# Layer 3's last mixture of experts: order of the last batch's routing and dense units, and bf16 products for its gate and up

## The chip, the core and the metric

The kernel runs on one core of a Trainium2 chip. The core has TensorE (PE, with its weight loads shown apart as PEld), VectorE (DVE), ScalarE (ACT), GpSimd (POOL) and SyncE (SP), each with an instruction queue of its own that runs in order. DMAs are issued by SP and by GpSimd. The metric is the device time of one execution in microseconds; lower is better.

## The reference

Four batches of 512 tokens, 128 wide, go through four layers of self-attention, cross-attention and a feed-forward part, each with a residual. The change concerns the last feed-forward part, a mixture of 32 experts of inner width 64, four per token, with a capacity of 256 rows per expert counted over all four batches in order, and one shared expert. Its weights are drawn as bf16 numbers.

```python
logits = (X @ gate_w.T).astype(jnp.float32)
scores = jax.nn.sigmoid(logits)
_, idx = jax.lax.top_k(scores + bias[None, :], K)
w = jnp.take_along_axis(scores, idx, axis=-1)
w = w / jnp.clip(jnp.sum(w, axis=-1, keepdims=True), 1e-12, None)
...
pos = jnp.take_along_axis(jnp.cumsum(onehot, axis=0) - 1, eid[:, None], axis=1)[:, 0]
valid = pos < C
...
h = jax.nn.silu(jnp.einsum('ecd,edi->eci', xe, W1)) * jnp.einsum('ecd,edi->eci', xe, W3)
ye = jnp.einsum('eci,eid->ecd', h, W2)
gflat = jnp.where(valid, w.reshape(-1), jnp.zeros((), x.dtype))
yrows = ye[eid, posc] * gflat[:, None]
out = yrows.reshape(-1, K, D).sum(axis=1)
out = out + jax.nn.silu(X @ sw1.T) * (X @ sw3.T) @ sw2.T
```

## The kernel before

Tokens are kept as rows (`x`, 128 partitions) and, after a layer norm, transposed in `xT` (128 x 512 per batch, `tokens(b)`). All products of this part are f32.

Batches 0, 1 and 2 go through **slots**. `route_slots` (L737) computes the routing on VectorE (`capped`, L686, with `router` and `topk`), and GpSimd scatters each token's row to its four experts' slots in DRAM, 16 indirect DMAs per batch (L776). This happens while the cross-attention before it still runs. `slot_experts` (L813) then fetches the slots of four half-experts at a time into SBUF: eight DMAs on SP (L825), which wait for all scatters. Eight rounds follow, each of four phases that lag behind each other: `turn` (four transposes, L830, and a ScalarE copy, L832), `inner` (four gate-and-up products at L425, SiLU on ScalarE at L846, a product on VectorE), `inner_turn` (two transposes, L854, a copy on VectorE, L856) and `down` (four products at L425, scaled by the token's weight on ScalarE, L870, and VectorE, L871). Each round ends in four indirect DMAs of GpSimd that scatter the rows back to a buffer `back` in DRAM (L873), 32 in all. `returned` (L912) fetches that buffer with three DMAs on SP (L919), adds the rows to `x` in 12 VectorE additions and stores each batch (L930). The shared expert of batches 0 to 2 is `shared_rows` (L895).

Batch 3 is **dense**: `ffn` (L951) runs every token through all experts, in 17 units of two experts each (the first unit is the shared expert). A unit is a gate and an up product (L425, to two PSUM banks `f`), SiLU on ScalarE (L1005), two VectorE products at L436 (by up, then by the routing weights spread over partitions), and, two units later, a down product (L1013) into the bank `acc`. The spread is a bf16 product of a pick matrix and the weights in three bf16 parts (`spread3`, L886); they come from `route_dense` (L717). PSUM has four banks `f`, one `acc`, three `s`.

The program is written as generators. `weave` (L390) steps one chain and takes a step of a second one every so many steps. Within what the program's order and dependencies leave open, a scheduler sets the order of each engine; inside `manual_schedule` the order of VectorE is the written one. In the last part the order is: shared rows of batches 0 and 1, then the rounds taking turns with the shared rows of batch 2, with batch 3's norm and routing woven in at one step per 2.2; then all 17 dense units, with the returned rows' additions woven in; then the last sums and batch 3's store (`out`, L2173).

Six weight packs hold gate, up and down of the 17 units as f32 in SBUF. Since the source in DRAM is bf16, `load` (L370) has GpSimd issue those DMAs, which convert; three of the six are in GpSimd's queue behind the scatters of batch 2. Loads without a conversion go to SP's queue. The room of the attention's tiles is given to this part once the attention is through.

Of the kernel before, what the change touches and what calls it, by code (L numbers as in the profile page):

```python
# [13 lines left out]
F32 = mybir.dt.float32  # L14
BF16 = mybir.dt.bfloat16
# [3 lines left out]
ALU = mybir.AluOpType  # L19
# [3 lines left out]
P = 128  # L23
B, S, D = 4, 512, 128
# [267 lines left out]
class Net:  # L292
# [74 lines left out]
    def acc(self, shape=(P, 512)):  # L367
        return self.bank("acc", shape)

    def load(self, name, pool, tag, cols=None):  # L370
        at, n = self.packs[name]
        src = self.dram[name]
        t = pool.tile([P, cols or n], F32, tag=tag, name="w_" + name.replace(".", "_"))
        cast = src.dtype != F32
        (self.nc.gpsimd if cast else self.nc.sync).dma_start(t[:, :n], src)
        return Weights(t, at)

# [275 lines left out]
    def spread(self, w, group, away, pool):  # L653

        nc = self.nc
        T, E = w.shape[1], w.shape[2]
        wp = pool.tile([P, T, E], F32, name="w_halves", tag="w_halves", bufs=1)
        nc.gpsimd.tensor_copy(
            wp.rearrange("p t (h u) -> p t h u", h=2), w.rearrange("p t (u h) -> p t h u", h=2)
        )  # L660
        yield
        for i, b in enumerate(group):
            t = self.sm((E, S))
            for j in range(TB):
                nc.tensor.transpose(t[:, j * P : j * P + P], wp[:, TB * i + j, :], self.ident)
            wT = pool.tile([E, S], F32, tag="w_turned", name="w_turned", bufs=2)
            self.move(wT, t)
            nc.sync.dma_start(away[b], wT)
            yield
# [16 lines left out]
    def capped(self, b, W, pool, m):  # L686
# [27 lines left out]
        nc.vector.scalar_tensor_tensor(fits, pp, float(CAP), hit, ALU.is_lt, ALU.mult)  # L714
        self.tt(w, w, fits, ALU.mult)

    def route_dense(self, b, W, pool):  # L717

        nc = self.nc
        E = 32  # L720
        m = {}
        yield from self.capped(b, W, pool, m)
        yield
        w3, rest = pool.tile([P, TB, 3, E], BF16, name="w3", bufs=1), pool.tile([P, TB, E], F32, name="w_rest", bufs=1)
        nc.vector.tensor_copy(w3[:, :, 0], m["w"])
        self.tt(rest, m["w"], w3[:, :, 0], ALU.subtract)
        nc.vector.tensor_copy(w3[:, :, 1], rest)
        self.tt(w3[:, :, 2], rest, w3[:, :, 1], ALU.subtract)
        yield
        t = self.bank("s", [3 * E, S], BF16)  # L730
        for j in range(TB):
            nc.tensor.transpose(t[:, j * P : j * P + P], w3[:, j].rearrange("p k e -> p (k e)"), self.identb)
        self.w3T = pool.tile([3 * E, S], BF16, name="w3T", bufs=1)
        nc.scalar.copy(self.w3T, t)
        yield
# [215 lines left out]
    def ffn(self, stage, group, E, base, pool, spread=None):  # L951

        nc = self.nc
        packs = self.units_of(stage, group)
        blocks = [packs[i : i + 2] for i in range(0, len(packs), 2)]
        away = self.chunks[stage] if not spread else None
        rest = [(b, [int(u) for u in routed]) for blk in blocks for b in group for _, _, routed in blk if routed]
        coming = []  # L960

        def chunk():

            if not rest or spread:
                return
            b, units = rest.pop(0)
            c = pool.tile([P, UNITS, S], F32, tag="c", name="c", bufs=3)
            for h in range(2):
                first = h * E // 2 + units[0]
                src = away[b, first : first + len(units)].rearrange("e s -> (e s)")  # L970
                nc.sync.dma_start(
                    c[64 * h : 64 * h + 64, : len(units)].rearrange("p e s -> p (e s)"), src.partition_broadcast(64)
                )
            coming.append(c)

        y = {b: pool.tile([P, S], F32, tag="y", name="y", bufs=4) for b in group}
        self.sums.update({(stage, b): y[b] for b in group})
        chunk()
        chunk()
        at = base  # L980
        for k, blk in enumerate(blocks):
            Ws = [self.pack(at + i, n) for i, (n, _, _) in enumerate(blk)]
            at += len(blk)
            ahead = at + len(blocks[k + 1]) - 1 if k + 1 < len(blocks) else at + 1
            for b in group:
                units = [(W, u, None) for W, (_, sh, _) in zip(Ws, blk) for u in sh]
                plan = []
                for W, (_, sh, routed) in zip(Ws, blk):
                    plan += [(W, u, None) for u in sh] + [(W, u, i) for i, u in enumerate(routed)]
                acc, cs = {}, {}  # L990
                for i, (W, u, in_c) in enumerate(plan):
                    if in_c is not None and spread:
                        if u not in cs:
                            cs.update(spread([v for _, v, in_c in plan[i : i + 2] if in_c is not None]))
                        cu = cs.pop(u)
                    elif in_c is not None:
                        if in_c == 0:
                            chunk()
                            c = coming.pop(0)
                        cu = c[:, in_c, :]  # L1000
                    pg, up = self.bank("f", (P, S)), self.bank("f", (P, S))
                    self.dot(pg, (W["g" + u], self.tokens(b)))
                    self.dot(up, (W["u" + u], self.tokens(b)))
                    h = pool.tile([P, S], F32, tag="h", name="h", bufs=5)
                    nc.scalar.activation(h, pg, AF.Silu)  # L1005
                    self.tt(h, h, up, ALU.mult)
                    if in_c is not None:
                        self.tt(h, h, cu, ALU.mult)

                    def down(W=W, u=u, h=h, i=i, b=b, acc=acc, n=len(plan), k=k):  # L1010
                        if i == 0:
                            acc["t"] = self.acc()
                        nc.tensor.matmul(acc["t"], lhsT=W["d" + u], rhs=h, start=i == 0, stop=i == n - 1)  # L1013
                        if i == n - 1 and k == 0:
                            nc.scalar.copy(y[b], acc["t"])
                        elif i == n - 1:
                            self.tt(y[b], y[b], acc["t"], ALU.add)

                    self.last.append(down)
                    if len(self.last) > 2:  # L1020
                        self.last.pop(0)()
                    if b == group[0] and i == 2:
                        self.want(ahead)
                    yield
# [13 lines left out]
    def l0_attn(self, pool, W, Wo):  # L1038
# [199 lines left out]
        def rounds(first, last):  # L1238
            n = len(items)
            item = lambda i: items[i] if 0 <= i < n else None  # L1240
            if first == 0:
                yield from project(0)
                load(0, 0)
                biases()
                load(0, 1)
                yield
# [932 lines left out]
def chained(*chains):  # L2179
    for c in chains:  # L2180
        yield from c


def some(steps, n):

    for _ in range(n):
        if next(steps, steps) is steps:
            return
        yield


def build(nc, packs, dram):
    first, second = GROUPS
    of = lambda stage: [n for n in packs if n.startswith(stage + ".") and n[-1].isdigit()]
    f2 = [f"l2_ffn.{kind}{hp}" for hp in range(8) for kind in ("qkv", "o")]
    feed = ["l0_attn.qk", "l0_attn.vo"]
    at = {}
# [6 lines left out]
    with tile.TileContext(nc) as tc, ExitStack() as ctx:  # L2204
        net = Net(ctx, tc, packs, dram, feed)
# [3 lines left out]
        def open_pool(name, right=False):  # L2209
            pools[name] = ExitStack()  # L2210
            return pools[name].enter_context(net.pool(name, right=right))
# [29 lines left out]
        ff = open_pool("ff")  # L2241
# [20 lines left out]
        y = {b: gates.tile([P, S], F32, name=f"y{b}") for b in range(B)}  # L2262
# [38 lines left out]
        dense = lambda b, fast=False: net.l2_dense(b, y[b], w4, s4, fast)  # L2301
# [17 lines left out]
        s5 = open_pool("s5", right=True)  # L2319
        x3 = open_pool("x3")  # L2320
# [15 lines left out]
        W5 = Both()  # L2336
# [11 lines left out]
        ff = open_pool("ff3")  # L2348
        banks(f=4, acc=1, s=3)
        net.want(at["l3"] + 2)  # L2350
        for i, n in enumerate(of("l3_ffn")):
            net.stay[n] = net.loaded[at["l3"] + i] if i < 3 else net.load(n, ff, f"w{i}")
        chain = chained(net.norm(3), net.route_dense(3, W5, s5))
        shared = [net.shared_rows(b, net.stay[of("l3_ffn")[0]], ff) for b in range(3)]
        net.weave(chained(shared[0], shared[1], net.turns(net.slot_experts(at["l3"], ff), shared[2])), chain, 2.2)
        with tc.manual_schedule(engines={mybir.EngineType.DVE}):
            back = net.returned(range(3), ff)
            next(back)
            net.weave(net.ffn("l3_ffn", (3,), 32, at["l3"], ff, net.spread3), back, 1.5, 6)
        net.flush()  # L2360
        for _ in net.out(3):
            pass
# [22 lines left out]
```

## Time and profile before

| What | us |
|---|---|
| median of three runs (2251.18 to 2261.61) | 2256.95 |
| the profiled execution, its own time | 2272.79 |
| its span, first to last instruction | 2271.0 |
| last scatter of batch 2 to the slots starts (L776) | at 2152.29 |
| first slot transposes on PE (L830) | at 2161.03 |
| first and last scatter back (L873) | at 2174.34 and 2224.72 |
| fetch of the returned rows (L919) | at 2226.86 |
| first store of the output (L930) | at 2243.07 |

Times of events are counted from the start of the span. A line number is that of the kernel before; L425 is `dot` and L436 `tt`, the helpers that record most products and most VectorE operations, so the tiles tell what such a row is: `f<-xT,w_l_ffn` is a gate or up product, `s<-w3T,pick` the spread, `acc<-h,w_l_ffn` the down product, `made` the scaled rows of a round. An f32 product of 512 columns appears as two MATMUL records, each with a weight load; a bf16 one as one. The ends of matmuls are modelled, so their starts are the safer measure. "Idle before" is the time in which an engine stood still ahead of an instruction, with what ended it; "remote" is a release whose source the profile doesn't know.

### The profile page before, as it was taken

What the parts mean: (1) busy time and instruction counts of PE and PEld (TensorE: products, weight loads), DVE (VectorE), ACT (ScalarE), POOL (GpSimd) and SP (SyncE); (2) the same over time, 40 slices, a digit from 0 to 9 for tenths busy, and PEclk for the clock granted to TensorE, in tenths of its full rate; (3) what the DMA queues carried; (4) which work ended last, traced back from release to release, by engine and by line L of the source; (5) the groups of instructions that cost most, each with busy time, mean ns of one, the idle gap of its engine ahead of it and who ended that gap; (6) DMA issues with size and microseconds to landing.
All of it is one profiled execution on the core that took longest, in us unless ns stands there. A gap on an engine that the chain in (4) does not pass through costs nothing.

```text
span 2271.0 us, 28138 instructions
## 1 busy us (share of the span) xinstructions
PE 2109.5 (93%) x8946; PEld 1121.5 (49%) x8946; DVE 1608.1 (71%) x4059; ACT 995.4 (44%) x2042; POOL 554.8 (24%) x695
## 2 busy tenths in 40 slices
PE   6999899999999998999999999999999996697778
PEld 3566556544545553444444544444444443564463
DVE  6667576666675769787977797867777765886525
ACT  4556446444325452444434543443343434364421
POOL 1000001000000001433323343333333322336541
PEclk7989999999999999999999999999999998898869
DMA  6321134254453344334334444444443442200022
GB/s 167 99 65 44 45 111 123 62 137 112 112 143 84 105 101 107 75 100 110 110 83 105 114 120 114 124 111 107 114 114 101 111 129 46 94 1 6 20 54 76
DMA packets 88947, 213.26 MB, mean 94 GB/s; under 512 B 21874, under 2 KB 40626, under 8 KB 88542
## 3 DMA queue, kind: packets, MB, share of 16 engines
q1 hardware_dynamic: 85230, 207.52, 34.9%
q0 software_dynamic: 3568, 3.93, 0.6%
q8 instruction: 71, 1.16, 0.2%
q14 instruction: 78, 0.64, 0.1%
HBM read 182.33 MB, written 23.53 MB: 91 GB/s over the span
## 4 chain that ended last, share of the span: by engine, by line
PE 72%; DVE 15%; issue 5%; ACT 3%; POOL 2%; DMA 2%; SPq 1%; another core or an unknown queue 0%; POOLq 0%; DVEq 0%; ACTq 0%
PE mm L425 19%; PE f L425 13%; PE mm L1854 8%; PE s L425 8%; PE acc L1013 6%; PE mm L1826 4%; PE mm L1801 4%; DVE h L436 2%; PE mm L1136 1%; PE mm L1203 1%; PE mm L1181 1%; DVE at_m L1883 1%; DVE m L1143 1%; DVE gvx L436 1%; PE s L515 1%
## 5 line engine op out<-in xcount | busy, mean ns | idle before, releaser
L1762 POOL TENSOR_TENSOR gvx<-gvx 128x512 f32<-128x512 f32 (+1 forms) x256 | 260.3, 1017 | 549.3 <-DVE gvx L436 488.3
L425 PE MATMUL f<-xT,w_l_ffn 128*128 128x512 f32 (+1 forms) x768 | 369.3, 603 | 1.2 <-ACT h L1005 0.7
L1885 ACT ACTIVATE at_e<-mm,at_m 128x512 f32<-128x512 f32 x256 | 173.0, 685 | 293.1 <-DVE at_m L1883 274.3
L425 PE MATMUL mm<-w_l_ffn_qkv,xT 128*128 128x512 f32 x512 | 266.3, 604 | 4.2 <-ACT at_e L1885 1.7
L1854 PE MATMUL mm<-og,w_l_ffn_o 128*128 128x512 f32 x512 | 265.8, 603 | 3.2 <-DVE og L436 3.2
L436 DVE TENSOR_TENSOR h<-h,f 128x512 f32<-128x512 f32 (+1 forms) x192 | 131.1, 684 | 139.9 <-PE f L425 105.3
L1005 ACT ACTIVATE h<-f 128x512 f32<-128x512 f32 x189 | 112.3, 596 | 251.0 <-PE f L425 214.2
L425 PEld LDWEIGHTS f<-xT,w_l_ffn 128*128 128x128 f32 (+1 forms) x768 | 140.2, 192 | 151.0 <-issue 123.6
L1013 PE MATMUL acc<-h,w_l_ffn 128*128 128x512 f32 x378 | 194.8, 600 | 3.5 <-DVE h L436 2.9
L436 DVE TENSOR_TENSOR gvx<-mm,gv 128x512 f32<-128x512 f32 x256 | 174.5, 683 | 20.8 <-PE mm L425 17.1
L436 DVE TENSOR_TENSOR og<-mm,c 128x512 f32<-128x512 f32 x256 | 176.2, 690 | 18.3 <-PE mm L1854 16.0
L1802 ACT COPY eT<-mm 128x512 f32<-128x512 f32 x256 | 137.6, 596 | 83.4 <-PE mm L1801 83.2
L1883 DVE TENSOR_REDUCE at_m<-mm 128x1 f32<-128x512 f32 x256 | 161.1, 681 | 11.7 <-PE mm L425 10.3
L1801 PEld LDWEIGHTS mm<-ident,at_e 128*128 128x128 f32 x1024 | 120.2, 142 | 68.4 <-issue 47.7
L1854 PEld LDWEIGHTS mm<-og,w_l_ffn_o 128*128 128x128 f32 x512 | 91.7, 191 | 114.4 <-issue 90.3
L1801 PE MATMUL mm<-ident,at_e 128*128 128x128 f32 x1024 | 135.1, 274 | 5.3 <-ACT at_e L1885 5.3
L425 PEld LDWEIGHTS mm<-w_l_ffn_qkv,xT 128*128 128x128 f32 x512 | 87.3, 190 | 95.2 <-issue 59.0
L425 PE MATMUL mm<-roped 64*128 64x512 f32 x512 | 131.3, 622 | 1.7 <-DVE roped L436 1.0
L1143 DVE TENSOR_REDUCE m<-mm 128x1 f32<-128x512 f32 (+3 forms) x176 | 104.8, 635 | 32.6 <-PE mm L1139 31.7
L1826 PE MATMUL mm<-eT,v 128*64 128x512 f32 x512 | 118.7, 599 | 0.0
L1013 PEld LDWEIGHTS acc<-h,w_l_ffn 128*128 128x128 f32 x378 | 71.2, 192 | 93.1 <-issue 67.3
L436 DVE TENSOR_TENSOR h<-h,c 128x512 f32<-128x512 f32 x160 | 111.5, 703 | 4.1 <-DMA c<-l_ffn_w 1.3
(453 smaller groups left out, 3529.4 us busy)
## 6 DMA issues: line engine op xcount, KB each, us to landing
c<-gates SPq DMA_DIRECT2D x256, 256.0 KB
c<-l_ffn_w SPq DMA_DIRECT2D x96, 384.0 KB
w_l_ffn<-in_l_ffn SPq DMA_DIRECT2D x26, 576.0 KB
w_l_ffn_qkv<-in_l_ffn_qkv SPq DMA_DIRECT2D x16, 640.0 KB
w_l_ffn_o<-in_l_ffn_o SPq DMA_DIRECT2D x16, 512.0 KB
rot<-qk SPq DMA_DIRECT2D x128, 64.0 KB
d<-inverted SPq DMA_DIRECT2D x64, 128.0 KB
k_parts<-k SPq DMA_DIRECT2D x12, 384.0 KB
```

The costliest lines, as they stand in the source:

```text
L425: self.nc.tensor.matmul(out, lhsT=lhsT, rhs=rhs, start=i == 0, stop=i == len(pairs) - 1)
L436: self.nc.vector.tensor_tensor(out, a, b, op)
L1005: nc.scalar.activation(h, pg, AF.Silu)
L1013: nc.tensor.matmul(acc["t"], lhsT=W["d" + u], rhs=h, start=i == 0, stop=i == n - 1)
L1143: nc.vector.tensor_reduce(m[:, i, h0 : h0 + per], ps, AX.X, ALU.max, negate=True)
L1762: nc.gpsimd.tensor_tensor(x[:, :, :m], x[:, :, :m], x[:, :, m : 2 * m], ALU.add)
L1801: nc.tensor.transpose(p[:, j, :], es[i][hl][:, j * P : j * P + P], self.ident)
L1802: nc.scalar.copy(eT[hl][:, :, i * P : i * P + P], p)
L1826: nc.tensor.matmul(po[64 * hl : 64 * hl + 64, :], lhsT=m["v"][:, j, hl, :], rhs=eT[hl][:, j, :], start=j == 0, stop=j == TB - 1,)
L1854: nc.tensor.matmul(acc, lhsT=W["o"][:, (e - 1) * D : e * D], rhs=hs.pop(e - 1), start=e == 1, stop=e == E)
L1883: nc.vector.tensor_reduce(m, s, AX.X, ALU.max, negate=True)
L1885: nc.scalar.activation(e[:, :n], s, AF.Exp, bias=m, accum_out=den)
```

## The change

`load` gets a type for its tile, so a pack can also be loaded as bf16 without a conversion. The six packs are loaded a second time in that way. A new function `tokens_in_three` splits batch 3's transposed tokens into three bf16 parts whose sum is the f32 value. For the dense units gate and up become three bf16 products each, of the bf16 weights with the three parts, accumulated in the same bank; down stays f32.

The order of the last part becomes: shared rows of batches 0 to 2 and three dense units, with norm, splitting and routing of batch 3 woven in at more than three steps per step; then the eight rounds, with seven dense units woven in at one per four steps; then the last seven units with the returned rows' additions. The tile `y` gets two buffers per batch of its group, which is two for batch 3 and four, as before, elsewhere.

```diff
-    def load(self, name, pool, tag, cols=None):
+    def load(self, name, pool, tag, cols=None, dt=F32):
         at, n = self.packs[name]
         src = self.dram[name]
-        t = pool.tile([P, cols or n], F32, tag=tag, name="w_" + name.replace(".", "_"))
-        cast = src.dtype != F32
+        t = pool.tile([P, cols or n], dt, tag=tag, name="w_" + name.replace(".", "_"))
+        cast = src.dtype != dt
         (self.nc.gpsimd if cast else self.nc.sync).dma_start(t[:, :n], src)
...
+    def tokens_in_three(self, b, pool):
+
+        nc = self.nc
+        self.x3 = x3 = pool.tile([P, 3, S], BF16, name="x3", bufs=1)
+        rest = pool.tile([P, S], F32, name="x_rest", bufs=1)
+        nc.scalar.copy(x3[:, 0], self.tokens(b))
+        self.tt(rest, self.tokens(b), x3[:, 0], ALU.subtract)
+        yield
+        nc.scalar.copy(x3[:, 1], rest)
+        self.tt(x3[:, 2], rest, x3[:, 1], ALU.subtract)
+        yield
...
-        y = {b: pool.tile([P, S], F32, tag="y", name="y", bufs=4) for b in group}
+        y = {b: pool.tile([P, S], F32, tag="y", name="y", bufs=2 * len(group)) for b in group}
...
+            names = {W: n for W, (n, _, _) in zip(Ws, blk)}
...
-                    self.dot(pg, (W["g" + u], self.tokens(b)))
-                    self.dot(up, (W["u" + u], self.tokens(b)))
+                    for ps, w in ((pg, "g"), (up, "u")):
+                        if spread:
+
+                            wb = self.in_bf16[names[W]][w + u]
+                            self.dot(ps, *[(wb, self.x3[:, i]) for i in range(3)])
+                        else:
+                            self.dot(ps, (W[w + u], self.tokens(b)))
...
-        chain = chained(net.norm(3), net.route_dense(3, W5, s5))
+        net.in_bf16 = {n: net.load(n, ff, f"b{i}", dt=BF16) for i, n in enumerate(of("l3_ffn"))}
         shared = [net.shared_rows(b, net.stay[of("l3_ffn")[0]], ff) for b in range(3)]
-        net.weave(chained(shared[0], shared[1], net.turns(net.slot_experts(at["l3"], ff), shared[2])), chain, 2.2)
+        chain = chained(net.norm(3), net.tokens_in_three(3, ff), net.route_dense(3, W5, s5))
+
+        dense = net.ffn("l3_ffn", (3,), 32, at["l3"], ff, net.spread3)
+        net.weave(chained(*shared, some(dense, 3)), chain, 0.3)
+        net.weave(net.slot_experts(at["l3"], ff), some(dense, 7), 4, 4)
         with tc.manual_schedule(engines={mybir.EngineType.DVE}):
             back = net.returned(range(3), ff)
             next(back)
-            net.weave(net.ffn("l3_ffn", (3,), 32, at["l3"], ff, net.spread3), back, 1.5, 6)
+            net.weave(dense, back, 1.0, 3)
```

`some(steps, n)` takes the next n steps of a generator; `chained` runs generators one after the other.

## The prediction

> **What bounds the kernel now.** I read the page's slices first: PE is busy nearly everywhere except in slices 36 to 39, the stretch that the change touches. Then I read that stretch by windows (columns: stretch and length, busy time and count of PE, weight loads, VectorE, ScalarE and GpSimd, granted clock, DMA share, GB/s):
>
> ```profile
> PEclk7989999999999999999999999999999998898869
> ...
> 2137.00:2154.00 17.00, 10.55 (x36) 4.73 (x34) 5.82 (x24) 4.12 (x8) 13.34 (x15) 0.87 0.02 0
> 2154.00:2161.00 7.00, 0.00 (x0) 0.00 (x0) 1.34 (x2) 0.93 (x2) 0.96 (x2) 0.50 1.08 336
> 2161.00:2174.00 13.00, 12.30 (x55) 11.13 (x56) 4.85 (x28) 5.67 (x10) 0.00 (x0) 0.52 0.49 119
> 2174.00:2213.00 39.00, 29.44 (x163) 23.10 (x162) 9.80 (x31) 10.24 (x27) 23.46 (x24) 0.74 0.03 7
> 2213.00:2227.00 14.00, 9.43 (x20) 4.18 (x20) 5.08 (x10) 2.42 (x5) 7.78 (x8) 0.76 0.03 6
> 2227.00:2271.00 44.00, 38.83 (x99) 16.87 (x97) 28.20 (x43) 8.35 (x14) 0.00 (x0) 0.98 0.28 96
> ```
>
> The 134 us from 2137 have no single bound. Until 2154 GpSimd issues batch 2's scatters; until 2161 PE stands still; then the slots' rounds run on a cold PE; from 2227 a warm PE runs the dense units. The timeline names the hand-overs (start, duration, engine, line, instruction, idle time before it and its releaser):
>
> ```profile
> 2152.29 0.97 POOL L776 DMA_INDIRECT slots<-sent,to  x1 [0.30 <-issue]
> ...
> 2161.03 1.12 PE L830 MATMUL f<-ident,slots 128*128 128x128 f32 x4 [10.19 <-DMA slots<-slots]
> ...
> 2174.34 1.04 POOL L873 DMA_INDIRECT back<-made,slots  x1 [19.38 <-ACT made L870]
> ...
> 2202.97 0.97 POOL L873 DMA_INDIRECT back<-made,slots  x1 [6.27 <-ACT made L870]
> ...
> 2222.17 0.97 POOL L873 DMA_INDIRECT back<-made,slots  x1 [2.89 <-DVE made L871]
> ...
> 2226.86 1.46 SPq L919 DMA_DIRECT2D back<-back  x3
> ```
>
> The end hangs on a chain: last scatter of batch 2, slots fetched, first round, 32 scatters back, fetch of the returned rows, the rest. The 32 scatters start 1.28 us apart where none waits, so they need 41.0; the two waits shown after the first scatter and one of 2.42 at 2186.78 cost 11.6 less three ordinary gaps of 0.3, or 10.7. The fetch leaves at 2226.86, and 44.1 us follow, because 16 of 17 dense units come after 2213:
>
> ```profile
> 2243.84 1.88 PE L425 MATMUL f<-xT,w_l_ffn 128*128 128x512 f32 x4
> 2245.55 1.02 PE L1013 MATMUL acc<-h,w_l_ffn 128*128 128x512 f32 x2
> 2246.41 0.60 PE L425 MATMUL s<-w3T,pick 96*128 96x512 bf16 x2
> 2246.84 1.88 PE L425 MATMUL f<-xT,w_l_ffn 128*128 128x512 f32 x4
> ```
>
> Start to start, gate and up take 1.71, the down product 0.86 and two bf16 spreads 0.43, so a bf16 pass of 512 columns is 0.215 and a unit is 1.71 + 0.86 + 0.22 = 2.79.
>
> **The change, part by part.** *Three parts.* Gate and up become six bf16 passes: 6 x 0.215 = 1.29, 0.43 less per unit, 7.3 us over 17. Only the units that stay behind the fetch can show it (7 x 0.43 = 3.0), and there VectorE takes over as the bound (below), so I count nothing. Making the parts costs two ScalarE copies (0.6 each, as L516's) and two VectorE subtractions (0.69, as L436's); the subtractions stand ahead of the top-k and put 1.4 us on the routing.
>
> *Six bf16 weight loads*, 768 + 5 x 1152 columns, 1.67 MB, on SP's queue ahead of the slots' fetch. Their room was the attention's, whose last readers on PE end at 2136.8 (L456). The returned rows, 3.1 MB, took some 10 us in the trace, so these take about 6 and land by 2145, while the DMA share is 0.02. Nothing is counted. If they started only with the fetch, the slots would be 6 us later: that is in the range. GpSimd's order does not change: its three f32 loads stay behind the scatters, at 2153.25.
>
> *Routing ahead of the rounds.* PE's order now holds all of the last batch's routing, the gate and up of units 0 to 2, two spreads and a down product before the first slot transposes (L830). PE is in order, so the rounds wait for the routing. I start it where the trace of before has the transposed tokens:
>
> ```profile
> 2153.75 0.59 ACT L516 COPY xT<-s 128x512 f32<-128x512 f32 x1 [7.11 <-remote]
> ```
>
> Its transposes were issued at 2146.93, yet ScalarE saw them 7 us later; such lateness of PE's results (6.49 and 5.08 at other places) occurs in the trace while GpSimd scatters, and I cannot name its cause. With it: xT at 2154.3; gate products 1.8 and sigmoid 0.3, 2156.4; bias, top-k and weights 3.8 (2166.34 to 2170.1) plus 1.4 of subtractions, 2161.6; place products 2.0 warm, 3.6 cold, 2164.5; gates of units 0 and 1 over the VectorE work, 2.6 warm, 5.2 cold, 2168; transposes, copy and the rest 3 to 4, 2171.5. Without the lateness all is 5 to 6 us earlier, 2166. I take the middle, **2169, 8 us later than the 2161.0 of before**.
>
> *First round.* Before, 13.3 us lay between the first slot transposes and the first scatter, with 3.8 us of gate and shared products in the way (2161.94 to 2165.63). Now two spreads and two down products are in the way (0.43 + 1.72 warm), and PE is warmer: 8 us if warm, 12 if cold. I take 9, nearer the warm end, since dense units run just before. First scatter at **2178**, 4 later than before.
>
> *Seven units among the rounds.* A round on PE is 1.09 + 0.64 + 0.28 + 0.45 = 2.5 warm, start to start (2176.70 on), so eight are 20; seven gate and up pairs 9.0, eight spreads 1.7, seven down products 6.0: 37 us at full clock. Here the Trainium skill has a rule ("TensorE: Matmul & The Clock Gate", Part 1): PE's default is half clock, a busy window of about 3.4 us releases it, an idle one takes it away. The row above has 0.74 in this stage, and the same eight products of a round take 1.16 warm and 2.07 at 2165.63. By the rule, with the gaps filled, 37 us; by the row 37 / 0.74 = 50. From 2169 the last down product is then at 2206 or 2219. GpSimd's own sum is 2178 + 41.0 = 2219, and it needs about 6 us after the last down product (2212 or 2225). So by the rule GpSimd is the bound; by the row PE just is. I take GpSimd's 2219 plus 3 of remaining waits: **last scatter 2222, fetch 2223**, 4 earlier than before although the first scatter is 4 later. VectorE per round is 0.4 + 0.4 + 0.6 + 1.4 = 2.8, ScalarE 0.6 + 0.4 + 0.6 + 0.6 = 2.2, both under GpSimd's 5.1, so four f and three s banks come free in time.
>
> A rule that speaks against the change is in "SBUF — State Buffer" (SBUF: two separate sides): GpSimd and VectorE share a port pair by exclusive lock[...]. The change puts some 10 us of VectorE work among the scatters. At 0.3 us lost per scatter that would be 10 us. But in the trace a scatter took 967 to 1135 ns, median 974, in all 48 of batches 0 to 2, of which batches 0 and 1 ran with VectorE over 60% busy (31.9 of the 50 us from 2050); I count nothing.
>
> *After the fetch.* Seven units' gates and nine down products are left: 9.0 + 1.3 + 7.7 = 18.0 of PE, half of it ahead of the returned rows. Rows of batch 0 land about 5 us after the fetch, all by 12. VectorE, whose order is written, has behind the first row addition 12 row additions, six of h, and two more: 20 x 0.72 = 14.4. Transposes and the wait for the last sums cost about 0.5, the last store 3.7 (2267.33 to 2271.0). So 5 + 14.4 + 0.5 + 3.7 = 23.6, say **23** instead of 44.1. This is the gain: nine units have left the tail.
>
> **Sum.** Span 2223 + 23 = 2246, against 2271.0: 25 us. The profiled execution took 2272.79, 15.8 above the median 2256.95 of the three runs; I take the difference off the median: 2257 - 25 = **2232**.
>
> **Rivals.** *Nothing is late* (0.16): xT is not held up and the rounds stay warm. Slots at 2163, first scatter 2171, last 2212, fetch 2213, span 2236, time 2222 or a little less. For it: the lateness falls on different instructions now. Against: it shows in every scatter burst. *Slots very late* (0.14): routing until 2173, 12 us of first round, then 14 us of waits as in before: scatters end 2240, span 2264, time 2250; within the noise. *Slower* (0.10): PE in order. It carries 37 us of work among the rounds; all cold it is 74, and 7 units add two hand-overs each to ScalarE and VectorE, late ones costing 2.4 to 7.1. From 2169 the last down product is then at 2243 plus lateness. It decides once that exceeds 9 us: the fetch passes 2259, the span 2282, time over 2268, about 2272. Against it: even all cold a round with its dense unit is about 9 us, and the dense work itself is what warms PE. That the bf16 weights come with the slots (the change not covering its loads) costs 6 and is in the second rival.
>
> **How the numbers follow.** The forecast itself has 0.60, with 2223 to 2245. Half a per cent, 11 us, is about what a measurement can tell from no change: 2245.7 to 2268. Faster is forecast plus first rival, 0.76; same 0.14; slower 0.10. The range 2216 to 2252 takes in the first rival and half of the second.
>
> **What would show it.** First slot transposes 2163 to 2173; the 32 scatters nearly without gaps, 41 to 47 us in all; the fetch at 2213 to 2230; then 22 to 25 us; granted clock over 0.85 in the rounds; gate and up at 1.29 per unit. Wrong if the scatters stretch over 55 us, if the slots' fetch leaves after 2157, or if the first round starts after 2176.

## The result, and the profile after

The changed kernel took **2249.27 us**, median of 20 runs, beside 2260.19 for the kernel before, run next to it (20 runs, 2251.18 to 2269.09). One of the 20 runs was disturbed and took 4208.78; the other 19 lie between 2237.61 and 2259.55, with a median of 2248.78, and the ratio is theirs. It is 0.9953, with a 95% interval from 0.9937 to 0.9969: some 11 us, where 25 were forecast. The time of 2232 was not reached by the median, nor by any single run; the median lies near the upper end of the range (2216 to 2252), where not the forecast but the second rival had put it.

The profiled execution of after took 2248.78, its span is 2247.0. The row of the granted clock on the page, and the same stretches by windows as were shown of before:

```profile
PEclk8999899999999999999999999999999999799888
```

```profile
2137.00:2154.00 17.00, 12.98 (x38) 5.04 (x36) 6.09 (x25) 7.26 (x13) 12.90 (x14) 0.80 0.22 70
2154.00:2161.00 7.00, 7.00 (x21) 4.31 (x20) 3.93 (x18) 3.65 (x5) 5.34 (x7) 0.50 0.18 47
2161.00:2174.00 13.00, 12.78 (x58) 7.25 (x59) 7.86 (x24) 2.96 (x5) 0.00 (x0) 0.84 0.98 275
2174.00:2213.00 39.00, 38.36 (x236) 25.20 (x240) 19.89 (x46) 17.54 (x40) 23.41 (x24) 1.00 0.03 7
2224.00:2247.00 23.00, 9.89 (x24) 3.49 (x21) 12.91 (x20) 1.19 (x2) 0.00 (x0) 0.71 0.53 182
```

From 2154 to 2161 PE is busy all the time, at half clock (0.50), where it stood still before, and in the rounds (2174 to 2213) it has full clock. Behind the fetch VectorE has more work than PE. The timeline names the hand-overs:

```profile
2157.58 0.97 POOL L788 DMA_INDIRECT slots<-sent,to  x1 [0.30 <-issue]
...
2172.49 0.60 PE L842 MATMUL f<-ident,slots 128*128 128x128 f32 x4
...
2179.67 1.04 POOL L885 DMA_INDIRECT back<-made,slots  x1 [19.42 <-ACT made L882]
...
2187.72 0.97 POOL L885 DMA_INDIRECT back<-made,slots  x1 [2.75 <-ACT made L882]
...
2222.17 0.97 POOL L885 DMA_INDIRECT back<-made,slots  x1 [0.30 <-DVE h L436]
...
2224.41 1.46 SPq L931 DMA_DIRECT2D back<-back  x3
...
2229.91 1.42 DVE L436 TENSOR_TENSOR x<-x,back 128x512 f32<-128x512 f32 x2 [8.05 <-DMA back<-back]
```

One wait of 2.75 and one of 0.70 are all that the 32 scatters lose, and 22.6 us follow the fetch: 5.5 until VectorE has the first rows, and 17.1 from there, on a chain that VectorE leads almost to the end. The last row shows a loss that the forecast's sum (5 + 14.4) contains without naming it. VectorE stands still for 8.05 us until the rows land, since its written order has the products of the remaining units behind the first row addition, and PE waits 5.39 us with it. What another order would bring there is untested.

The end at 2247.0 is almost the forecast 2246, but by luck. The stretch before these lines ended 5.3 us later than in the profile of before (last scatter to the slots at 2157.58 against 2152.29), and what follows was 4.3 us shorter than forecast. So from here on times are counted from the start of that scatter; the stretch from it to the end is called the tail. It is 89.4 us after and 118.7 in the first profile of before: 29 us less, of which the runs show 11. The experiments ask where the rest is.

### The profile page after: what moved, and what is told of

Read it like the earlier page. It is cut to its first block, busy times and chain, and to the rows that moved or that the text cites. A ratio compares the mean times of both kernels' runs of the same rounds, so it can differ in the third digit from the quotient of the medians.

```text
span 2247.0 us, 28205 instructions
## 1 busy us (share of the span) xinstructions
PE 2100.3 (93%) x8974; PEld 1112.3 (50%) x8980; DVE 1608.4 (72%) x4061; ACT 998.2 (44%) x2044; POOL 555.1 (25%) x695
## 4 chain that ended last, share of the span: by engine, by line
PE 72%; DVE 17%; issue 4%; ACT 3%; POOL 2%; DMA 2%; SPq 0%; DVEq 0%; ACTq 0%; POOLq 0%
PE mm L425 19%; PE f L425 13%; PE s L425 8%; PE mm L1873 8%; PE acc L1032 6%; PE mm L1845 5%; PE mm L1820 4%; DVE h L436 2%; PE mm L1200 1%; PE mm L1155 1%; PE mm L1222 1%; DVE m L1162 1%; DVE at_m L1902 1%; PE acc L2183 1%; PE s L515 1%
## 5 line engine op out<-in xcount | busy, mean ns | idle before, releaser
L425 PE MATMUL f<-xT,w_l_ffn 128*128 128x512 f32 (+1 forms) x700 | 338.4, 605 | 1.2 <-ACT h L1024 0.7
L425 PEld LDWEIGHTS f<-xT,w_l_ffn 128*128 128x128 f32 (+1 forms) x700 | 126.9, 192 | 132.9 <-issue 111.2
L436 DVE TENSOR_TENSOR gvx<-mm,gv 128x512 f32<-128x512 f32 x256 | 174.8, 685 | 22.2 <-PE mm L425 18.6
```

The source lines that it names most:

```text
L425: self.nc.tensor.matmul(out, lhsT=lhsT, rhs=rhs, start=i == 0, stop=i == len(pairs) - 1)
L436: self.nc.vector.tensor_tensor(out, a, b, op)
```

## The experiments

**Is the profile of before at fault, or the stretch ahead?** Two kernels: before again, and a head without the last mixture of experts.

```diff
-        ff = open_pool("ff3")
...
-        for _ in net.out(3):
-            pass
+        for b in range(B):
+            net.store(b)
```

> The kernel before, unchanged. Theory A (the profiled execution of before had an unusual tail): its profiled execution now comes near the median, 2255 to 2265, and from batch 2's last scatter to the end lie 103 to 110 us instead of 118.7, with fewer long hand-overs. Theory B (the profiler itself slows this tail): profiled 2268 to 2276 again, tail 116 to 120, while the timed runs stay at 2260. Theory C (the tail is always 118, the stretch ahead of it varies): profiled near 2260 with a tail of 117 to 120 and the last scatter of batch 2 at 2140 to 2145.

> Layer 3's last mixture of experts is left out behind batch 2's scatters, and the tokens are stored as they are. Its instruction order up to there is that of before. Last scatter of batch 2 in the profile at 2152 plus or minus 4. Theories A and B: timed runs of 2155 to 2160, so that before's tail is 2260 less that, 100 to 105. Theory C: timed runs of 2143 to 2148, which leaves a tail of 113 to 118.

Before again: 2261.91 (2250.79 to 2271.30), ratio 1.0002. Its profiled execution took 2261.95, with a tail of 99.2. Head: 2163.82 (2159.91 to 2167.95); in its profile 6.0 us lie behind the last scatter and 1.85 around the span, which puts that scatter at 2156.0 in the median and leaves a tail of 2259.73 - 1.8 - 2156.0 = 102. So theory B falls, the profiler doesn't stretch the tail, and C falls, the head doesn't hide 15 us. The tail of 118.7 is not that of the runs on this chip. This is the new profile of before, windows and timeline of PE:

```profile
2169.70:2182.70 13.00, 12.31 (x55) 11.06 (x56) 4.86 (x28) 5.61 (x9) 0.00 (x0) 0.51 0.49 118
2182.70:2202.70 20.00, 17.93 (x142) 14.73 (x140) 8.33 (x28) 8.95 (x24) 15.01 (x16) 1.00 0.04 9
2202.70:2222.70 20.00, 20.00 (x64) 9.30 (x63) 10.44 (x21) 5.58 (x13) 15.26 (x16) 1.00 0.04 8
2225.00:2260.20 35.20, 28.73 (x73) 12.08 (x71) 23.03 (x35) 5.38 (x9) 0.00 (x0) 0.96 0.34 120
```

```profile
2203.07 1.02 PE L425 MATMUL f<-xT,w_l_ffn 128*128 128x512 f32 x2
...
2207.24 3.60 PE L425 MATMUL f<-xT,w_l_ffn 128*128 128x512 f32 x8
```

The first round is as cold as in the profile shown before the prediction (0.51), and the first scatter back comes 22.1 us behind the last one to the slots in both. But then the clock is 1.00, not 0.74. The 32 scatters have no gap (39.7 us from first to last, against 50.4), PE is at the dense units at 2203, some 20 us before the last scatter, and eight of them have had their gate and up products when the fetch leaves at 2224.98; 35.2 us follow, not 44.1.

**The parts alone**, on the same chip as these two:

> The new order alone: gate and up stay f32, and neither the six bf16 loads nor the three parts are there. If the order brings the whole gain and the loads cost nothing: 2247 to 2252, as the changed kernel. If the bf16 loads cost some 5 us ahead of the slots: 2242 to 2246. If the shorter products bring a part: 2252 to 2258.

> The bf16 products and their loads in the order of before. 17 units of 0.43 us less are 7.3 at most: 2253 to 2257 if the dense units of this tail are bound by TensorE and the loads are free; 2258 to 2262 if VectorE or the returned rows hide it; 2263 to 2267 if the loads cost 5 us ahead of the slots.

```diff
# order_f32
-                        if spread:
...
+                        self.dot(ps, (W[w + u], self.tokens(b)))
...
-        net.in_bf16 = {n: net.load(n, ff, f"b{i}", dt=BF16) for i, n in enumerate(of("l3_ffn"))}
-        chain = chained(net.norm(3), net.tokens_in_three(3, ff), net.route_dense(3, W5, s5))
+        chain = chained(net.norm(3), net.route_dense(3, W5, s5))
...
# bf16_old_order
-        net.weave(net.slot_experts(at["l3"], ff), some(dense, 7), 4, 4)
+        net.weave(chained(shared[0], shared[1], net.turns(net.slot_experts(at["l3"], ff), shared[2])), chain, 2.2)
...
-            net.weave(dense, back, 1.0, 3)
+            net.weave(net.ffn("l3_ffn", (3,), 32, at["l3"], ff, net.spread3), back, 1.5, 6)
```

Order alone: 2254.41, ratio 0.9968 (0.9954 to 0.9983). Products alone: 2252.55, ratio 0.9970 (0.9956 to 0.9984). Each brings about 0.3% of the 0.47% that both bring, so they overlap in part; and the loads cost nothing that shows. The forecast had counted the products at nothing. In the one profile of the products alone the tail is 93.8, or 5.4 us less than in before_again: 2.0 of them lie behind the fetch, and 3.6 in the first round, where PE was back at full clock after 5 us instead of 12. Whether the products brought that too is not shown; below, the same program has 12 us in one execution and 6 in another.

**Is it the units' place?**

```diff
-        net.weave(net.slot_experts(at["l3"], ff), some(dense, 7), 4, 4)
+        net.weave(net.slot_experts(at["l3"], ff))
...
-            net.weave(dense, back, 1.0, 3)
+            net.weave(dense, back, 1.5, 6)
```

With 14 units left behind the rounds, the additions of the returned rows are also woven in more thinly.

> The changed kernel, unchanged. Theory A (a single profiled execution is one draw out of a spread of some 20 us, and before's was an extreme one): timed 2249 plus or minus 2, profiled anywhere between 2238 and 2260; the tail from batch 2's last scatter to the end is again 86 to 92 us, since this order leaves TensorE no long stand-still in which it could go cold. Theory C (the changed kernel is 5 us later ahead of its tail, because of its loads): the last scatter of batch 2 again at 2157 or later, and over 3 us later than in the order with f32 (2155.4) and in before (2152.3 and 2161.0).

> The changed kernel, but no dense unit among the slots' rounds: all 14 that are left come behind them. By the step on record (nine units leave the tail, 44 becomes 23 behind the fetch) the tail behind the fetch is then 38 to 42 us and the time 2260 to 2266, with the fetch a little earlier. If in ordinary executions the units' place hardly matters, because TensorE takes them early anyway: 2249 to 2254.

After again: 2250.22, ratio 0.9954 (0.9938 to 0.9970), tail 88.1. None among the rounds: 2250.88, ratio 0.9963 (0.9946 to 0.9980). The place of the seven units is not to be told from no change, where the step on record wanted 10 to 16 us. Its timeline of PE shows why:

```profile
2199.66 1.68 PE L425 MATMUL f<-x,w_l_ffn 128*128 128x512 bf16 x7
...
2208.51 1.46 PE L425 MATMUL f<-x,w_l_ffn 128*128 128x512 bf16 x6
2209.80 1.02 PE L1032 MATMUL acc<-h,w_l_ffn 128*128 128x512 f32 x2
```

PE needs about 2.5 us for a round, GpSimd 5.1. With nothing between them PE is through with the rounds at about 2199 and runs units in the time in which GpSimd still scatters, to 2217.72. By the fetch at 2219.96, 10 of the 14 later units have had their gates; 27.8 us follow it, not 38. VectorE stands still there too, 9.23 us ahead of the first row addition. The scatters are gapless (39.7 us). "Behind the rounds" in the program's order was never "behind the fetch" in time. The rows also show the forecast 1.29 from the gates to the down product.

**Does the cold first round cost?** Two orders with the slot transposes ahead of the routing, and two with products whose results are unused, to fill PE's wait for the slots:

```diff
# slots_first
+        net.weave(chained(shared[0], shared[1], net.turns(some(slots, 13), shared[2])), chain, 1.2)
+        net.weave(slots, some(dense, 10), 2.0, 0)
...
# one_ahead
+        net.weave(chained(*shared), chained(net.norm(3), net.tokens_in_three(3, ff)), 1.0)
+        for _ in some(dense, 1):
+            pass
+        net.weave(some(slots, 13), net.route_dense(3, W5, s5), 1.0)
+        net.weave(slots, some(dense, 9), 2.2, 0)
...
# before_warm, behind the shared rows of batches 0 and 1
+            for _ in range(10):
+                nc.tensor.matmul(t, lhsT=w["gs0"], rhs=net.tokens(0), start=True, stop=True)
...
# one_ahead_warm, ahead of the slots
+        for _ in range(24):
+            nc.tensor.matmul(fill, lhsT=wb, rhs=net.x3[:, 0], start=True, stop=True)
```

> The bf16 parts, units among the rounds, but the first slot transposes stand on TensorE ahead of the last batch's routing, as before the change, and no dense unit ahead of them. If the routing ahead of the rounds holds them up (first scatter back 22 us behind the last scatter to the slots in the changed kernel, 18.6 in the old order with bf16): first scatter back after 18 to 20 us, rounds nearly gapless (40 to 43), 23 to 25 behind the fetch, tail 83 to 88, time 2242 to 2247. If the routing among the rounds makes waits instead: 2248 to 2254.

> As the run before it, but all shared rows, the gates of the routing and one dense unit's gate and up stand ahead of the first slot transposes, in the time in which TensorE waits for the slots. 2241 to 2246 if this time is free; 2247 to 2251 if these products come late and hold up the first round.

> The kernel before, with ten more f32 products of 512 columns on TensorE (8.6 us at full clock, results unused) in the time in which it waits for the slots. If the stand-still of 10 us sends it into the rounds at half clock, and this costs before its time: granted clock over 0.9 behind the slots, first scatter back 15 to 18 us behind the last scatter to the slots instead of 22.1, tail 92 to 96, time 2252 to 2256. If the clock comes back by itself at no cost to the end: 2257 to 2262. If the products run late and hold up the first transposes: 2262 to 2268.

> The order with one dense unit ahead of the slots, with 24 more bf16 products of 512 columns (5.2 us at full clock, results unused) in TensorE's wait for them. If a cold TensorE is why its first scatter back comes 22.1 us behind the last scatter to the slots: 16 to 18, the rounds 40 to 43, 22 to 24 behind the fetch, tail 82 to 87, time 2240 to 2244. If not: 2247 to 2251.

| Kernel | median, us | ratio (95%) | first scatter back | scatters | behind the fetch | tail |
|---|---|---|---|---|---|---|
| slots_first | 2249.80 | 0.9962 (0.9947 to 0.9976) | +21.8 | 44.3 | 22.8 | 91.1 |
| one_ahead | 2247.27 | 0.9949 (0.9932 to 0.9966) | +22.1 | 43.1 | 22.5 | 90.0 |
| before_warm | 2254.25 | 0.9973 (0.9955 to 0.9992) | +17.8 | 39.7 | 35.1 | 94.7 |
| one_ahead_warm | 2251.05 | 0.9958 (0.9940 to 0.9976) | +18.9 | 43.1 | 22.8 | 87.0 |

(The last four columns are of one profiled execution each.) In slots_first and one_ahead the slots are transposed 8.4 to 8.9 us behind the last scatter, as early as they land, and 6 us earlier than in the changed kernel; yet the first scatter back is no earlier. By windows, PE in one_ahead, the first three rows of 4, 4 and 5 us from the first transposes, and in before_warm the wait and the same three:

```profile
2162.84:2166.84 4.00, 4.00 (x19) 4.00 (x20) 0.00 (x0) 0.59 (x1) 0.00 (x0) 0.50 1.21 294
2166.84:2170.84 4.00, 4.00 (x17) 3.48 (x17) 1.35 (x5) 0.97 (x2) 0.00 (x0) 0.50 0.32 75
2170.84:2175.84 5.00, 5.00 (x25) 4.02 (x25) 1.44 (x5) 1.35 (x4) 0.00 (x0) 0.59 0.02 3
```

```profile
2166.90:2175.90 9.00, 8.41 (x20) 3.10 (x19) 0.48 (x1) 0.59 (x1) 2.60 (x4) 1.00 0.88 270
2175.90:2179.90 4.00, 3.98 (x32) 3.67 (x32) 1.56 (x7) 3.27 (x4) 0.00 (x0) 1.00 1.21 294
2179.90:2183.90 4.00, 2.53 (x22) 2.11 (x21) 3.40 (x22) 1.99 (x5) 0.00 (x0) 1.00 0.31 75
2183.90:2188.90 5.00, 4.27 (x35) 3.55 (x34) 1.56 (x5) 2.04 (x6) 3.34 (x4) 1.00 0.03 5
```

The clock is the last column but two. In these profiles of slots_first and one_ahead, and in every profile of before, PE has stood still for 5 us or more and then runs the first 12 us at half clock, although it is busy. In before_warm, kept busy, it has full clock, and before's first scatter back comes 4.3 us earlier. The whole kernel gains 5.9 by it (1.8 to 10.2 by the interval), as expected.

The 12 us are no constant. A second profile of one_ahead, the run one_ahead_2 further down, has stood still for 6.38 us (5.65 in one_ahead), is back at full clock after 6, and has its first scatter back at +19.1 without any filling:

```profile
2164.95:2168.95 4.00, 4.00 (x19) 4.00 (x20) 0.00 (x0) 0.58 (x1) 0.00 (x0) 0.50 1.21 295
2168.95:2172.95 4.00, 4.00 (x24) 3.52 (x24) 1.70 (x6) 0.97 (x2) 0.00 (x0) 0.75 0.42 101
```

So the +18.9 of one_ahead_warm can't be put down to its 24 products. Its time of 2240 to 2244 was missed (2251.05), and its profiled execution (2246.05) is the fastest of its runs. What filling is worth in this order stays open.

**Is the long tail one late hand-over?** In the first profile of before, one copy of the slots was 2.44 us late and the clock fell behind it.

```diff
...
-            nc.scalar.copy(xT, t)
+            nc.scalar.copy(xT, t if q != 4 else t.unsqueeze(1).to_broadcast([P, 4, 4, P])); xT = xT if q != 4 else xT[:, 0]
```

In the fifth round the copy writes the slots four times over, to a tile of its own; the first copy of them is used.

> The kernel before, but in the fifth round ScalarE's copy of the transposed slots is one four times as wide (128x2048, some 2.2 us instead of 0.6), so that TensorE gets it about as late as in the first profiled execution of before, where one copy was 2.44 us late and the granted clock then fell to 0.5 for 18 us. If one such hand-over is enough for the long tail: clock at 0.5 for 10 us or more behind it, two or three waits of the scatters with 5 to 11 us in all, 38 to 45 us behind the fetch, tail 107 to 119, time 2266 to 2276. If it takes more than one: no wait of the scatters over 2 us, tail 98 to 103, time 2257 to 2263.

> The kernel before a third time, for its profile. If the long tail of the first profiled execution is rare: 97 to 102 us from batch 2's last scatter to the end, no wait of the scatters, 34 to 36 us behind the fetch. If it is common: 108 or more in this one too.

Late: 2278.41, before on the same chip 2279.90 (27 runs, 2269.73 to 2288.45), ratio 0.9992 (0.9979 to 1.0006). On this chip before takes 20 us more than on the chips of the other runs (2257.6 to 2260.2), and its own profile there has the tail of 118.0, with waits at the same scatters as in the first profile. The edit therefore says nothing: the late hand-overs were there without it. What the pair shows is that the long tail goes with the **chip**, or with the occasion: each chip of this case was used in one set of runs only, so the two are not told apart. ScalarE's copy of the fifth round's slots, on this chip and in before_again on the other:

```profile
2180.25 0.59 ACT L832 COPY slotsT<-f 128x512 f32<-128x512 f32 x1 [2.35 <-remote]
```

```profile
2188.17 0.59 ACT L832 COPY slotsT<-f 128x512 f32<-128x512 f32 x1 [0.24 <-PE f L830]
```

**Does the change gain 25 us on such a chip?** The changed kernel ran beside before on four more chips, of which the last is such a one.

> The changed kernel, unchanged, beside before, on whichever chip it comes to. The tail of before is 99 us on one chip and 118 to 120 on another, where TensorE's results reach ScalarE late at the same instructions each time and before takes 2280. If the chip is the whole difference: where before takes 2275 or more the changed kernel gains 20 to 30 us, since its last scatters have no such waits; where before takes 2260 it gains 9 to 12. If the late hand-overs hit the new order as hard: 9 to 12 us on either kind of chip.

> The changed kernel beside before, on whichever chip it comes to. If the chip is the whole difference: a gain of 20 to 30 us where before takes 2275 or more, and of 9 to 12 where before takes 2260. If the late hand-overs hit the new order as hard: 9 to 12 us on either kind.

> The changed kernel, beside before and beside the order with one dense unit ahead, on one chip. Where before takes 2275 or more: a gain of 20 to 30 us if that chip's late hand-overs are the whole difference, 9 to 12 if they hit the new order too. Where before takes 2260: 9 to 12 again.

> The order with one dense unit ahead of the slots, again. If its 2247.3 of the run before was a gain over the changed kernel: 2 to 4 us under the changed kernel on the same chip. If it was spread: within 1.5 us of it.

> The kernel before a fourth time, for its profile. If the kind of chip sets its tail: 97 to 102 us with no wait of the scatters where before takes 2260, and 116 to 120 with the same three waits where it takes 2275 or more. If executions of one chip differ so: either, whatever the chip.

> The changed kernel beside it. Where before takes 2275 or more: a gain of 20 to 30 us if that chip's late hand-overs are the whole difference, 9 to 12 if they hit the new order too. Where before takes 2260: 9 to 12.

| Runs | before, us | after, us | ratio (95%) | tail before | tail after |
|---|---|---|---|---|---|
| after_third | 2259.00 | 2250.11 | 0.9955 (0.9942 to 0.9969) | | 89.3 |
| after_fourth | 2257.59 | 2248.95 | 0.9953 (0.9937 to 0.9970) | | 89.3 |
| after_fifth | 2258.94 | 2248.19 | 0.9942 (0.9919 to 0.9964) | | 89.5 |
| after_sixth | 2279.44 | 2266.67 | 0.9937 (0.9915 to 0.9960) | 118.9 (before_look_2) | 103.4 |

one_ahead_2, on after_fifth's chip, had 2245.02 and 0.9946 (0.9925 to 0.9966). Its median lies 3.2 us under that of the changed kernel, as expected of a gain, but its ratio is no lower: nine runs of each don't tell them apart, so no order tried here beats the changed kernel beyond doubt. The last row is the second chip on which before takes 2279. There the gain is 12.8 us (9 to 19 by the interval, from six runs), far from 25, because the late hand-overs hit the new order too. First its before, then the changed kernel, the scatters that waited over 2 us:

```profile
2180.97 1.04 POOL L873 DMA_INDIRECT back<-made,slots  x1 [19.57 <-ACT made L870]
...
2193.39 0.97 POOL L873 DMA_INDIRECT back<-made,slots  x1 [2.40 <-ACT made L870]
...
2209.57 0.97 POOL L873 DMA_INDIRECT back<-made,slots  x1 [6.26 <-ACT made L870]
...
2228.78 0.97 POOL L873 DMA_INDIRECT back<-made,slots  x1 [2.90 <-DVE made L871]
```

```profile
2185.56 1.04 POOL L885 DMA_INDIRECT back<-made,slots  x1 [25.59 <-ACT made L882]
...
2193.60 0.97 POOL L885 DMA_INDIRECT back<-made,slots  x1 [2.75 <-ACT made L882]
...
2206.30 0.97 POOL L885 DMA_INDIRECT back<-made,slots  x1 [2.58 <-ACT made L882]
...
2214.50 0.97 POOL L885 DMA_INDIRECT back<-made,slots  x1 [3.41 <-ACT made L882]
...
2226.78 0.97 POOL L885 DMA_INDIRECT back<-made,slots  x1 [2.15 <-ACT made L882]
```

Compare the first line of each with the last scatter to the slots, at 2158.73 and 2157.30: the first scatter back comes at +22.2 before and +28.3 after. The routing that now stands ahead of the rounds takes the lateness on itself: its scores reach the top-k at +7.2 (2164.48), where in the first profile of after they do at +1.2, and the slot transposes follow 6.2 us later than there (+21.1, +14.9). From first to last the scatters take 50.4 before and 50.1 after.

## Why the prediction was wrong

By stretches of the tail, with the forecast's own numbers counted from its 2152.3 (us; chip a: a chip on which before takes 2260, chip b: 2280; each column of measured numbers is one profile):

| | forecast, before | forecast, after | a: before | a: after | b: before | b: after |
|---|---|---|---|---|---|---|
| to the first scatter back | 22.1 | 25.7 | 22.1 | 22.1 | 22.2 | 28.3 |
| first to last scatter | 50.4 | 44 | 39.7 | 42.5 | 50.4 | 50.1 |
| last scatter to fetch | 2.1 | 1 | 2.1 | 2.2 | 2.1 | 2.3 |
| fetch to end | 44.1 | 23 | 35.2 | 22.6 | 44.1 | 22.8 |
| tail | 118.7 | 93.7 | 99.2 | 89.4 | 118.9 | 103.4 |

**The step that failed** is the subtraction, "25 us; I take the difference off the median: 2257 - 25". Its first term, 118.7, is a tail of chip b; its second, 93.7, is near the 89.4 of chip a and far from the 103.4 of chip b, since "GpSimd's 2219 plus 3 of remaining waits" supposes hand-overs that are no longer late. On one and the same chip the tail shrinks by 9.8 us (a) or 15.5 (b), and the medians by 8 to 11 or 12.8. That the profiled execution lay 15.8 us above the median stood in the text and was put aside as an offset common to both kernels; it sat in the very stretch that the change touches. The profile of before agrees line by line with chip b and not with a, while the runs beside it (2251 to 2262) are those of chip a; this match is how I read it, since the chip of that profile isn't known.

**"44.1 us follow, because 16 of 17 dense units come after 2213"** was read as the program's order. It was the lateness of PE in that execution: on chip a eight units have had their gates at the fetch, so the tail behind it falls by 12.6, not 21. That this stretch ends at 22.6 after the change (23 forecast, VectorE the bound) was right on both chips. none_among adds that the place of the seven units among the rounds is not the cause: without it 27.8 us follow the fetch, 7.4 less than before, and the fetch leaves so much earlier that the tail is 90.5.

**Waits of the scatters.** "The two waits... cost 10.7": none on chip a, where the change makes the scatters 2.8 us longer. On b they stay. The forecast took lateness as something that the new order escapes; its rival "slots very late" had the waits (scatters to 2240, time 2250) and came close to the median, but for chip a by another way.

**Routing ahead of the rounds.** On chip a the first slot transposes come at +14.9 (+16.7 forecast, with xT held up) and the first scatter back at +22.1 (+25.7). The later start was right in direction and nearly in size. The 4 us of delay for the first scatter did not come, since a PE at full clock (1.00) takes 7.2 us for the first round where 9 was said. There the routing gives back on PE's clock what it loses in time: slots_first transposes 6 us earlier and scatters no earlier. It need not be so in each execution, as one_ahead_2 shows (+19.1). On b the routing costs 6.1.

**Rule or row for the clock.** In the rounds of after the granted clock is 1.00 on chip a, as the rule of "TensorE: Matmul & The Clock Gate" would have it. But before has 1.00 there too, until 2203 without any dense unit; the row of 0.74 goes with chip b, where the stretch of the 32 scatters has 0.73 before and 0.86 after. The choice between them cost nothing. In the first round the rule of a busy window of about 3.4 us does not hold: one_ahead's PE is busy without a gap for 12 us at 0.50.

**Costed at nothing.** The bf16 loads: slots' fetch 2.15 us behind the last scatter before and after (2154.44 and 2159.73), right. The shared port that the prediction weighed: a scatter takes 972 ns median after, 974 before, with VectorE busy 19.9 instead of 9.8 of the 39 us in the rounds, right. The products: 0.3% when alone, about 0.15% (0.9968 to 0.9953, intervals overlapping) on top of the order, a small gain where none was counted.

**The signs.** Those listed for the profile of after held: first slot transposes at 2172.49, scatters of 42.5 us, the fetch at 2224.41, then 22.6, a clock of 1.00, gates at 1.29. Of the signs of being wrong one appeared, a slots' fetch after 2157 (2159.73), but only because the last scatter itself came late. All of them test the second term of the subtraction; none tested the first, which was the one at fault.

**Slips in the sums.** Starts of 32 scatters 1.28 us apart span 39.7 us, not 41.0; the 1 us from the last scatter to the fetch, which takes 2.1, makes up for most of it. The products in the way of the first round took 3.7 us (2161.94 to 2165.63), not 3.8.

## What to carry to other kernels

Before an expected gain is taken off a profile, hold the profiled execution against the timed runs: if it lies outside them, find the stretch in which it is longer, and don't subtract in that stretch. Count times from an event that the change doesn't touch, here the last scatter, since up to there the profiles of this case lie up to 16 us apart (2150.5 to 2166.8). Work that stands behind another engine's queue in the program may already run beside it: see when the engine that does it comes free, not where its lines stand. And let one of the signs to be looked for test the starting point of the forecast, not only the profile after the change.

## What the runs showed of the hardware

In two of nine sets of runs the same kernel was 20 us slower (2279.9 and 2279.4 against 2257.6 to 2260.2), and the profiles put all of it into the tail (118.0 and 118.9 against 99.2): up to 2137 they agree (PE busy 2008.4 to 2009.3 us on both kinds). In the tail, while GpSimd scatters to DRAM, ScalarE waits 2 to 6 us longer for results of PE (2.35 us against 0.24 for the slots of the fifth round, 3.43 to 7.11 against 1.08 for the transposed tokens), and three profiles of before have the same three waits of the scatters. In all three, PE stands still for 2.0 to 2.1 us behind the late slots, and 1 to 2 us later it is at half clock, for some 20 us (before_look: 0.66, 0.50, 0.50 and 0.88 in four windows of 7 us from 2180); before_again has neither. Why the results are late there stays open.

The length of half clock behind a stand-still differs between executions of one program, 12 us in one_ahead and 6 in one_ahead_2, and so does the first scatter back (+22.1, +19.1).

On one chip the time of a run goes with its mean granted clock: over 14 runs of before_again, which spread over 20 us, the correlation is -0.95, with 2.0 us for each 0.001 of clock. Which of the two follows the other is not shown.
